# Biases and second weights of a 48-expert layer: VectorE adds the second bias, the second weights are read in 512-byte runs, six sets of weights

## The chip, the cores and the metric

The kernel runs on one core of a Trainium2 chip. A core has five engines that work side by side, each on its own queue of instructions in order: TensorE (PE, matmuls; its weight loads are shown apart as PEld), VectorE (DVE), ScalarE (ACT), GpSimd (POOL) and SyncE (SP, which only issues transfers here). Sixteen DMA engines move data between HBM and SBUF. The engines meet by semaphores. The metric is the device time of one execution in microseconds (us), as the median of several runs; lower is better.

## The reference, cut to what matters

The model is a stack of four layers, each an attention-like block and a feed-forward block, with a layer norm around each. The change lies in the feed-forward block of the second layer, a mixture of experts in which each of 48 experts picks its own 128 of 4096 tokens of width 256:

```python
E, S, D, M = (48, 4, 256, 256)      # W1: (E, S, D, M), b1: (E, S, M), W2: (E, S, M, 64), b2: (E, S, 64)
logits = xf @ Wr.T
vals, idx = jax.lax.top_k(logits.T, cap)          # cap = 128
w = jax.nn.softmax(vals, axis=-1)
xg = xf[idx]
h = jax.nn.gelu(jnp.einsum('ecd,esdm->ecsm', xg, W1) + b1[:, None], approximate=False)
y = jnp.einsum('ecsm,esmk->ecsk', h, W2) + b2[:, None]
y = y.reshape(E, cap, D) * w[..., None]
out = jnp.zeros_like(xf).at[idx.reshape(-1)].add(y.reshape(-1, D))
```

All of it is in float32. Each expert has four slices (S). A slice takes all 256 inputs to 256 hidden units, and these to its own 64 of the 256 outputs. So the first weights of an expert are 1 MB and the second 256 KB.

## The kernel before, in words

`tile_sandwich_kernel` runs the layers one after another over 8 sequences of 512 tokens, `X`, which stay in SBUF. Tiles come from pools. A pool with `bufs=n` hands out n buffers in turn for each tag, and an instruction that writes a buffer waits until the last readers of its former contents are done. The order on each engine's queue is made by a scheduler from the program and these dependences. Transfers on one queue are issued in that order, so one that waits holds up those behind it.

The routing runs inside the attention block of the same layer (`class Choice`). For each sequence `logits` normalizes the tokens, writes them to HBM as `xn_d` (L1156) and multiplies them by the router. `lists` sorts each expert's best tokens and writes them to HBM as `tab_d` (L1195). `l1_ffn` does this for the last sequence, number 7, then calls `slots`. That merges the sorted lists on VectorE: offsets `ati` (L1272), ownership masks `own` (L1290 to L1293), five indirect loads `win` from `tab_d` issued by GpSimd (L1277), products `v` (L1299 to L1302), and small matmuls `pgot` that give the token numbers `iT` and weights `wT` of all experts (L1307, L1309).

Then comes the loop over the 48 experts, in which every engine has a part:

- SP issues the loads of the expert's first weights `w1` (L1350), second weights `w2` (L1351) and second bias `b2` (L1352) into one of three sets of buffers. In `w1` the 256 inputs lie on 128 partitions in two halves `c`. In `w2` the 256 hidden units lie on the partitions in the same way, unit c x 128 + p on partition p, so that a run of consecutive bytes in HBM is one row of 64 numbers, 256 bytes.
- GpSimd issues the indirect load of the 128 tokens, `xg` (L1354).
- PE transposes them into PSUM, `pxg` (L1359), and VectorE copies them to SBUF, `xgT` (L1361).
- PE multiplies: 16 matmuls give the hidden units `h`, eight blocks of 128 units by 128 tokens, four in each half (L1368). In the trace a float32 matmul is two PE instructions with a weight load each, a transpose is one. The stationary side of a matmul (`lhsT`) is loaded first and is called the weights by PE; here it is a block of `w1`.
- ScalarE adds the first bias and applies gelu, `hT` (L1373). The bias is a column of `b1`, which lies in the layer's slot of small weights; the slot is handed to the next layer's feed-forward weights `l2f_gu` (L250) once `b1` is no longer read. These are integers, which VectorE turns into floats in six pieces (L1798).
- PE starts the output `y` with a matmul of a row of ones and the row `b2`, which sets the bias in all 256 columns (L1377), and adds eight matmuls of 64 columns (L1379), two for each slice.
- VectorE multiplies by the tokens' weights, `yw` (L1383), and GpSimd issues an indirect transfer that adds the 128 rows to `out_d` in HBM (L1384).

After the experts `l2_attn` begins: `late` loads the sums of a sequence back as `yl` (L1504) and adds them to `X`. Its tiles take the SBUF space of the experts' pools, and its first instructions (L1420, L1429, L1442) wait for the last of the transfers that add rows.

Of the kernel before, what the change touches and what calls it, by code (L numbers as in the profile page):

```python
# [9 lines left out]
F32 = mybir.dt.float32  # L10
# [4 lines left out]
ALU = mybir.AluOpType  # L15
# [4 lines left out]
P = 128  # L20
# [3 lines left out]
D = 256  # L24
# [1080 lines left out]
class Choice:  # L1105
# [7 lines left out]
    E, NL, K = 48, 10, 128  # L1113
# [212 lines left out]
def l1_ffn(K):  # L1326
    nc, tc = K.nc, K.tc
    b1 = K.W["l1_ffn"][:, 96:480]
    ch, i = K.choice, K.i
    E = ch.E  # L1330
    with ExitStack() as es:
        es.enter_context(ch.es)

        def pool(name, bufs, **kw):
            return es.enter_context(tc.tile_pool(name="f1" + name, bufs=bufs, **kw))
        cst = pool("c", 1)
        wp = pool("w", 3)
        sb = pool("s", 2)
        pmm = pool("pm", 2, space=PSUM)
        pH = pool("ph", 4, space=PSUM)  # L1340
        pY = pool("py", 2, space=PSUM)
        ch.logits(NB - 1, sb, pmm, "mm")
        for _ in ch.lists(len(ch.GROUPS) - 1):
            pass
        wT, iT = ch.slots(cst, sb, pmm, "mm")
        for e in range(E):
            w1 = wp.tile([P, 4, 2, D], F32, tag="w1", name=f"w1_{e}")
            w2 = wp.tile([P, 4, 2, 64], F32, tag="w2", name=f"w2_{e}")
            b2 = wp.tile([1, D], F32, tag="b2", name=f"b2_{e}")
            nc.sync.dma_start(out=w1, in_=i["l1f_w1"][e].rearrange("s (c p) m -> p s c m", p=P))  # L1350
            nc.sync.dma_start(out=w2, in_=i["l1f_w2"][e].rearrange("s (c p) k -> p s c k", p=P))  # L1351
            nc.sync.dma_start(out=b2, in_=i["l1f_b2"][e:e + 1, :])  # L1352
            xg = sb.tile([P, D], F32, tag="xg", name=f"xg{e}")
            nc.gpsimd.indirect_dma_start(  # L1354
                out=xg, out_offset=None, in_=ch.xn_d[:, :],
                in_offset=bass.IndirectOffsetOnAxis(ap=iT[:, e:e + 1], axis=0))
            ps = pmm.tile([P, 2, P], F32, tag="mm", name=f"pxg{e}")
            for c in range(2):
                nc.tensor.transpose(ps[:, c, :], xg[:, c * P:(c + 1) * P], K.ident)  # L1359
            xgT = sb.tile([P, 2, P], F32, tag="xgT", name=f"xgT{e}")  # L1360
            nc.vector.tensor_copy(xgT, ps)  # L1361
            hT = sb.tile([P, 8, P], F32, tag="hT", name=f"hT{e}")
            for half in range(2):
                ph = pH.tile([P, 4, P], F32, tag="h", name=f"h{e}_{half}")
                for j in range(4):
                    s, m = 2 * half + j // 2, j % 2
                    for c in range(2):
                        nc.tensor.matmul(  # L1368
                            ph[:, j, :], lhsT=w1[:, s, c, m * P:(m + 1) * P],
                            rhs=xgT[:, c, :], start=(c == 0), stop=(c == 1))  # L1370
                for j in range(4):
                    q = 4 * half + j
                    nc.scalar.activation(  # L1373
                        hT[:, q, :], ph[:, j, :], AF.Gelu,
                        bias=b1[:, 8 * e + q:8 * e + q + 1])
            py = pY.tile([P, D], F32, tag="y", name=f"y{e}")
            nc.tensor.matmul(py, lhsT=K.ones, rhs=b2, start=True, stop=False)  # L1377
            for q in range(8):
                nc.tensor.matmul(  # L1379
                    py[:, (q // 2) * 64:(q // 2 + 1) * 64], lhsT=hT[:, q, :],  # L1380
                    rhs=w2[:, q // 2, q % 2, :], start=False, stop=(q == 7))
            yw = sb.tile([P, D], F32, tag="yw", name=f"yw{e}")
            nc.vector.tensor_scalar(yw, py, wT[:, e:e + 1], None, ALU.mult)  # L1383
            nc.gpsimd.indirect_dma_start(  # L1384
                out=ch.out_d[:, :],
                out_offset=bass.IndirectOffsetOnAxis(ap=iT[:, e:e + 1], axis=0),
                in_=yw, in_offset=None, compute_op=ALU.add)

    def late(b, pool):
        y = pool.tile([P, NT, D], F32, tag="xn", name=f"yl{b}")  # L1390
        nc.sync.dma_start(
            out=y, in_=ch.out_d[b * L:(b + 1) * L].rearrange("(n p) d -> p n d", p=P))
        K.add_norm(b, [y[:, n, :] for n in range(NT)], pool, parts=2)


    K.late = late
# [847 lines left out]
def l3_ffn(K):  # L2244
# [18 lines left out]
    with ExitStack() as es:  # L2263
# [295 lines left out]
        for b in range(NB):  # L2559
# [11 lines left out]

LAYERS = (("l0_attn", load_l0_attn, l0_attn), ("l0_ffn", load_l0_ffn, l0_ffn),
          ("l1_attn", load_l1_attn, l1_attn), ("l1_ffn", load_l1_ffn, l1_ffn),
          ("l2_attn", load_l2_attn, l2_attn), ("l2_ffn", load_l2_ffn, lambda K: None),
          ("l3_attn", load_l3_attn, l3_attn), ("l3_ffn", lambda K: None, l3_ffn))
# [94 lines left out]
```

## Time and profile before

| what | value |
|---|---|
| median of 3 runs | 4558.23 us (4555.81 to 4564.57) |
| the profiled execution | 4555.24 us |
| its span, first to last instruction | 4553.5 us |
| granted PE clock, mean | 0.930 |
| PE busy | 3963.8 us (87%) |
| weight loads on PE busy | 2633.7 us (58%) |
| VectorE busy | 2698.8 us (59%) |
| ScalarE busy | 2016.2 us (44%) |
| GpSimd busy | 2118.9 us (47%) |
| `h` matmuls of the experts (L1368) | 1536 instructions, 185.0 us |
| `y` matmuls of the experts (L1379) | 768 instructions, median 275 ns |
| bias matmuls of the experts (L1377) | 96 instructions, median 375 ns |
| loads of `w1` and `w2` | 48 x 1024 KB and 48 x 256 KB |

The shares of the span are averages over all layers, and each layer has its own limit. The change touches a stretch of some 300 us, and what it is worth has to be read there. Matmuls are pipelined, so their durations overlap: 275 ns each at a pace of about 110. The distance from one weight load to the next says more than the mean duration. A wait is named by the instruction that waited, and by what ended the wait. In a line of the timeline the columns are the start, the length of the group, engine, line, operation, written tile <- read tiles, shape, and how many instructions were merged. "issue" is idle time in which an engine waited for nothing that the profile shows. The strip of the DMA engines gives the busy share in tenths, with packet times that overlap counted twice.

### The profile page before, as it was taken

The numbers are of one execution on the slowest core, as the hardware profiler recorded it, in microseconds if no ns is written. First come the engines' busy times: TensorE is split into PE (matmuls) and PEld (weight loads), VectorE is DVE, ScalarE is ACT, GpSimd is POOL, SyncE is SP. The second block draws the span as 40 slices with busy tenths as digits, with TensorE's granted clock in tenths as the row PEclk, the third lists the DMA queues.
The fourth block names the chain that finished last, engine by engine and source line by source line (L and its number), as shares of the span: only waits on it lengthen the run. The fifth ranks groups of instructions, "written<-read, shape, count | busy, mean of one in ns | idle before, by whom it ended". The sixth has DMA issues, their size and how long they took to land. (4 is left out here: it accounts for less than half of the span.)

```text
span 4553.5 us, 63426 instructions
## 1 busy us (share of the span) xinstructions
PE 3963.8 (87%) x21672; PEld 2633.7 (58%) x21672; DVE 2698.8 (59%) x7145; ACT 2016.2 (44%) x4210; POOL 2118.9 (47%) x2081
## 2 busy tenths in 40 slices
PE   8868888999998599699999978998888876899997
PEld 3435765555655499544554534565655545678884
DVE  7767656456757611255566534888888899721115
ACT  5532433444344233334444444767676655311112
POOL 0045222444344244344555423889988879223321
PEclk9889999999999799889999989899999886899999
DMA  4377621000000299400000002343433334336653
GB/s 120 94 218 189 179 62 63 5 5 7 7 10 16 69 254 251 130 5 10 6 6 6 1 23 68 123 125 126 127 122 122 124 110 136 103 118 234 228 180 113
DMA packets 392818, 442.90 MB, mean 97 GB/s; under 512 B 147853, under 2 KB 275967, under 8 KB 391983
## 3 DMA queue, kind: packets, MB, share of 16 engines
q1 hardware_dynamic: 361087, 390.18, 28.4%
q0 software_dynamic: 16272, 31.87, 2.6%
q10 hardware_dynamic: 15136, 16.80, 1.1%
q8 instruction: 172, 2.82, 0.3%
q14 instruction: 151, 1.24, 0.1%
HBM read 372.49 MB, written 66.26 MB: 96 GB/s over the span
## 5 line engine op out<-in xcount | busy, mean ns | idle before, releaser
L2085 POOL TENSOR_TENSOR h<-h,C 128x1024 f32<-128x1024 f32 x256 | 613.3, 2408 | 135.3 <-DVE h L2081 87.8
L2081 DVE TENSOR_TENSOR_SCAN h<-dA,dB 128x512 f32<-128x512 f32 x480 | 568.4, 1209 | 90.2 <-ACT dA L2069 73.9
L1039 POOL TENSOR_SCALAR p<-p,rs 128x128 f32<-128x128 f32 (+3 forms) x256 | 275.8, 1085 | 417.3 <-DVE rs L1038 261.1
L2069 ACT ACTIVATE dA<-dl,A 128x512 f32<-128x512 f32 x480 | 330.3, 690 | 174.4 <-DVE h L2081 173.7
L1605 DVE CUSTOM_DVE_ANT_0 junk<-S,mask 128x256 f32<-128x256 f32 (+3 forms) x512 | 249.5, 487 | 195.0 <-PE S L1599 156.7
L2098 PE MATMUL y<-C,h 128*128 128x128 f32 x2048 | 298.4, 297 | 68.0 <-POOL h L2085 67.9
L2098 PEld LDWEIGHTS y<-C,h 128*128 128x128 f32 x2048 | 263.2, 155 | 155.3 <-POOL h L2085 98.6
L1633 ACT ACTIVATE PT<-T 128x128 f32<-128x128 f32 (+3 forms) x512 | 198.0, 435 | 278.5 <-PE T L1628 267.6
L1599 PE MATMUL S<-KZ,QT 64*128 64x512 f32 (+3 forms) x1024 | 260.9, 492 | 23.9 <-DVE mx L1605 23.6
L2297 PE MATMUL gb<-xbT,w_b 128*128 128x256 f32 (+1 forms) x1472 | 255.3, 332 | 1.0 <-ACT ts L2501 0.6
L2297 PEld LDWEIGHTS gb<-xbT,w_b 128*128 128x128 f32 x1472 | 230.4, 191 | 22.8 <-ACT ts L2501 0.8
L2303 DVE TENSOR_TENSOR hTb<-sb,gb 128x512 f32<-128x512 f32 x71 | 48.8, 687 | 325.4 <-PE gb L2297 325.4
L2064 POOL TENSOR_TENSOR dB<-du,B 128x1024 f32<-128x1024 f32 x96 | 234.0, 2437 | 0.1
L1883 PE MATMUL pf<-fT,w_l_ffn 128*128 128x512 f32 x384 | 208.3, 681 | 26.5 <-ACT fT L1877 10.4
L1628 PE MATMUL T<-QT,KZ 64*128 64x384 f32 (+3 forms) x1024 | 216.7, 464 | 2.9 <-ACT PT L1633 2.5
L2064 DVE TENSOR_TENSOR dB<-du,pb 128x1024 f32<-128x1024 f32 x160 | 191.2, 1195 | 23.0 <-ACT pb L2062 21.2
L182 POOL TENSOR_TENSOR X<-X,yn 128x256 f32<-128x256 f32 (+1 forms) x56 | 79.4, 1436 | 255.3 <-ACT yn L177 213.9
L1373 ACT ACTIVATE hT<-h,w_l_ffn 128x128 f32<-128x128 f32 x384 | 109.5, 368 | 197.9 <-PE h L1368 197.9
L1368 PE MATMUL h<-xgT,w 128*128 128x128 f32 x1536 | 185.0, 279 | 0.0
L1636 POOL TENSOR_SCALAR_AFFINE_SELECT PT<-PT 128x512 f32<-128x512 f32 x128 | 81.2, 634 | 219.8 <-ACT PT L1633 206.8
L1599 PEld LDWEIGHTS S<-KZ,QT 64*128 64x128 f32 x1024 | 117.2, 193 | 113.9 <-issue 58.4
L2534 POOL DMA_INDIRECT ys<-yb,place x71 | 69.8, 984 | 238.7 <-ACT yb L2533 224.5
(605 smaller groups left out, 9266.5 us busy)
## 6 DMA issues: line engine op xcount, KB each, us to landing
w_b<-l3f_w SPq DMA_DIRECT2D x138, 512.0 KB
C<-xdd SPq DMA_DIRECT2D x256, 256.0 KB
B<-xdd SPq DMA_DIRECT2D x256, 256.0 KB
w<-l1f_w SPq DMA_DIRECT2D x48, 1024.0 KB
w<-l1f_w SPq DMA_DIRECT2D x48, 256.0 KB
band<-l0fd SPq DMA_DIRECT2D x30, 320.0 KB
X<-x SPq DMA_DIRECT2D x16, 512.0 KB
c<-ys SPq DMA_DIRECT2D x16, 512.0 KB
```

What stands on the lines that cost most here:

```text
L1039: nc.gpsimd.tensor_scalar(p[:, 0:n], p[:, 0:n], rs, None, ALU.mult)
L1599: nc.tensor.matmul(ps[:, 0:n], lhsT=QT[half, qt * P:n], rhs=KZ[half, j % 2, 0:n], start=True, stop=True)
L1605: nc.vector.tensor_tensor_reduce(out=junk[:, 0:n], in0=ps[:, 0:n], in1=mask[:, L - n:L], scale=1.0, scalar=-3.0e38, op0=ALU.add, op1=ALU.m ...
L1628: nc.tensor.matmul(ps[:, 0:n], lhsT=KZ[half, j % 2, kt * P:(kt + 1) * P], rhs=QT[half, kt * P:L], start=True, stop=True)
L1633: nc.scalar.activation(PT[:, j, :], ps[:, 0:n], AF.Exp)
L1883: nc.tensor.matmul(ps, lhsT=gu[:, k, j * 768 + c * P:j * 768 + (c + 1) * P], rhs=R[b]["fT"][:, k, :], start=(k == 0), stop=(k == 1))
L2064: on.tensor_tensor(dBs[k], R[b]["du", h], B[:, None, :].to_broadcast([P, 2, L]), ALU.mult)
L2069: nc.scalar.activation(dA, R[b]["dl", h][:, c, :], AF.Exp, scale=A[:, 2 * h + c, n:n + 1])
L2081: nc.vector.tensor_tensor_scan(hs[k][:, c, :], dA, dBs[k][:, c, :], 0.0, ALU.mult, ALU.add)
L2085: nc.gpsimd.tensor_tensor(hs[k], hs[k], row_C.pop(k)[:, None, :].to_broadcast([P, 2, L]), ALU.mult)
L2098: nc.tensor.matmul(R[b]["y", h][q // 2][:, q % 2, c * P:(c + 1) * P], lhsT=t[:, c, q * P:(q + 1) * P], rhs=K.ident, is_transpose=True, sta ...
L2297: nc.tensor.matmul(ps[:, q, :], lhsT=ww[:, k, (c + q) * P:(c + q + 1) * P], rhs=xT[:, k, :], start=(k == 0), stop=(k == 1))
```

## The change

Five edits, all in `l1_ffn`:

- The pool of the experts' weights has six sets of buffers in place of three.
- The second weights are loaded as `(p c) k`: hidden units 2p and 2p + 1 lie on partition p, and their two rows of 64 numbers are one run of 512 bytes.
- For this the blocks of hidden units change: block m of a slice has units m, m + 2, m + 4 and so on. So the `h` matmuls take every second column of `w1` as weights, `m::2`, and the first bias has to be rearranged in the same way. Two tiles do that once, before the loop: `turn`, made of the even or odd columns of the identity matrix on GpSimd, and `bq`, the rearranged bias, made by four matmuls with `turn` on PE (the tiles `pbq`) and two copies on ScalarE.
- The second bias is loaded into all 128 partitions, 128 KB in place of 1 KB. The matmul with the row of ones is gone; each pair of matmuls of a slice now starts and ends its own sum in PSUM.
- VectorE adds the bias from SBUF to `y` (`tensor_tensor`), and multiplies by the tokens' weights in a second instruction.

```diff
@@ -1334,7 +1334,7 @@
         def pool(name, bufs, **kw):
             return es.enter_context(tc.tile_pool(name="f1" + name, bufs=bufs, **kw))
         cst = pool("c", 1)
-        wp = pool("w", 3)
+        wp = pool("w", 6)
         sb = pool("s", 2)
         pmm = pool("pm", 2, space=PSUM)
         pH = pool("ph", 4, space=PSUM)
@@ -1342,14 +1342,27 @@
         ch.logits(NB - 1, sb, pmm, "mm")
         for _ in ch.lists(len(ch.GROUPS) - 1):
             pass
+        turn = cst.tile([P, 2, 2, P], F32, name="turn")
+        nc.gpsimd.memset(turn, 0.0)
+        bq = cst.tile([P, 4 * E, 2], F32, name="bq")
+        for c in range(2):
+            for half in range(2):
+                nc.gpsimd.tensor_copy(
+                    turn[:, c, half, 64 * half:64 * half + 64], K.ident[:, c::2])
+            pb = pmm.tile([P, 4 * E], F32, tag="mm", name=f"pbq{c}")
+            for half in range(2):
+                nc.tensor.matmul(
+                    pb, lhsT=turn[:, c, half, :], rhs=b1[:, half::2],
+                    start=(half == 0), stop=(half == 1))
+            nc.scalar.copy(bq[:, :, c], pb)
         wT, iT = ch.slots(cst, sb, pmm, "mm")
         for e in range(E):
             w1 = wp.tile([P, 4, 2, D], F32, tag="w1", name=f"w1_{e}")
             w2 = wp.tile([P, 4, 2, 64], F32, tag="w2", name=f"w2_{e}")
-            b2 = wp.tile([1, D], F32, tag="b2", name=f"b2_{e}")
+            b2 = wp.tile([P, D], F32, tag="b2", name=f"b2_{e}")
             nc.sync.dma_start(out=w1, in_=i["l1f_w1"][e].rearrange("s (c p) m -> p s c m", p=P))
-            nc.sync.dma_start(out=w2, in_=i["l1f_w2"][e].rearrange("s (c p) k -> p s c k", p=P))
-            nc.sync.dma_start(out=b2, in_=i["l1f_b2"][e:e + 1, :])
+            nc.sync.dma_start(out=w2, in_=i["l1f_w2"][e].rearrange("s (p c) k -> p s c k", c=2))
+            nc.sync.dma_start(out=b2, in_=i["l1f_b2"][e].partition_broadcast(P))
             xg = sb.tile([P, D], F32, tag="xg", name=f"xg{e}")
             nc.gpsimd.indirect_dma_start(
                 out=xg, out_offset=None, in_=ch.xn_d[:, :],
@@ -1366,21 +1379,21 @@
                     s, m = 2 * half + j // 2, j % 2
                     for c in range(2):
                         nc.tensor.matmul(
-                            ph[:, j, :], lhsT=w1[:, s, c, m * P:(m + 1) * P],
+                            ph[:, j, :], lhsT=w1[:, s, c, m::2],
                             rhs=xgT[:, c, :], start=(c == 0), stop=(c == 1))
                 for j in range(4):
                     q = 4 * half + j
                     nc.scalar.activation(
                         hT[:, q, :], ph[:, j, :], AF.Gelu,
-                        bias=b1[:, 8 * e + q:8 * e + q + 1])
+                        bias=bq[:, 4 * e + q // 2, q % 2:q % 2 + 1])
             py = pY.tile([P, D], F32, tag="y", name=f"y{e}")
-            nc.tensor.matmul(py, lhsT=K.ones, rhs=b2, start=True, stop=False)
             for q in range(8):
                 nc.tensor.matmul(
                     py[:, (q // 2) * 64:(q // 2 + 1) * 64], lhsT=hT[:, q, :],
-                    rhs=w2[:, q // 2, q % 2, :], start=False, stop=(q == 7))
+                    rhs=w2[:, q // 2, q % 2, :], start=(q % 2 == 0), stop=(q % 2 == 1))
             yw = sb.tile([P, D], F32, tag="yw", name=f"yw{e}")
-            nc.vector.tensor_scalar(yw, py, wT[:, e:e + 1], None, ALU.mult)
+            nc.vector.tensor_tensor(yw, py, b2, ALU.add)
+            nc.vector.tensor_scalar(yw, yw, wT[:, e:e + 1], None, ALU.mult)
             nc.gpsimd.indirect_dma_start(
                 out=ch.out_d[:, :],
                 out_offset=bass.IndirectOffsetOnAxis(ap=iT[:, e:e + 1], axis=0),
```

## The prediction

> **What bounds the kernel now.** I read the page first (the order by time and the strip of slices), then the stretch in which the 48 experts run, by engine. The stage runs from about 1579 us (first `h` matmul) to 1882 us (last `y`), 303 of the 4553.5 us of the span. Busy time by engine in its middle (the columns are the stretch, its length, then busy us of PE, weight loads, VectorE, ScalarE, GpSimd, then clock, DMA share, GB/s):
>
> ```profile
> core 0: us, PE busy (x) PEld busy (x) DVE busy (x) ACT busy (x) POOL busy (x), PEclk, DMA share, GB/s
> 1600.00:1850.00 250.00, 250.00 (x2068) 232.30 (x2067) 35.41 (x78) 91.23 (x320) 101.50 (x79) 1.00 0.95 251
> ```
>
> PE never rests, and the DMA engines read 0.95: two candidates for the bound. Who waits for whom tells them apart. In the waits of that stretch no PE instruction waits for a weight load, and the SP queue's own waits from 1440 to 1900 us show the opposite, loads waiting for PE to free one of three buffers:
>
> ```profile
> SPq L1350 <- PE h L1368: 149.7, 45, 31.3
> ```
>
> The DMA share adds packet times that overlap. One period of 6.30 us, by packets, and two short stretches in it that hold one kind alone (1 KB runs of `w1`; 256-byte runs of `w2`):
>
> ```profile
> DMA  9577799999999999999998999999999996410014
> ```
> ```profile
> DMA packets 602, 0.62 MB, mean 385 GB/s; under 512 B 0, under 2 KB 602, under 8 KB 602
> ```
> ```profile
> DMA packets 592, 0.17 MB, mean 278 GB/s; under 512 B 591, under 2 KB 591, under 8 KB 591
> ```
>
> The strip has a hole at the end of each period, and 1 KB runs move at 385 GB/s where the mean is 251. So PE's order sets the period. One expert on the weight-load queue (start, length, row):
>
> ```profile
> 1703.45 1.20 PEld L1379 LDWEIGHTS y<-w,hT 128*128 128x128 f32 x10
> 1704.52 0.20 PEld L1359 LDWEIGHTS pxg<-C,xg 128*128 128x128 f32 x1
> 1704.63 0.31 PEld L1379 LDWEIGHTS y<-w,hT 128*128 128x128 f32 x2
> 1704.80 0.19 PEld L1359 LDWEIGHTS pxg<-C,xg 128*128 128x128 f32 x1
> 1705.12 0.29 PEld L1377 LDWEIGHTS y<-b,ones 1*128 1x128 f32 x2
> 1705.74 0.52 PEld L1379 LDWEIGHTS y<-w,hT 128*128 128x128 f32 x4 [0.33 <-issue]
> 1706.18 3.65 PEld L1368 LDWEIGHTS h<-xgT,w 128*128 128x128 f32 x32
> ```
>
> The reader is to see the pace, 32 loads in 3.57 us (1706.18 to 1709.75), 0.11 us each whether the matmul behind has 128 or 64 columns, and the one break in it: from the second `pxg` load to the next `y` load takes 0.94 us, with only the bias pair in between.
>
> **The change, part by part.**
>
> *Bias matmul off PE.* Without L1377 the `y` load would follow `pxg` after 0.11 us: 0.94 - 0.11 = 0.83 us an expert. The biases of experts 0 and 1 ran early (1513.8), outside the stage, so 46 experts: 46 x 0.83 = 38.2 us, all on the path.
>
> *What is late next.* In the instruction order of the changed kernel the experts go in pairs: both pairs of transposes sit in the tail of the odd expert's `y`. From the second `pxg` load of the even expert to its first `h` load lie six loads, 0.66 us. `xgT` needs 0.43 until VectorE starts (1704.80 to 1705.23 here), 0.42 to copy and some 0.05 to be seen: 0.90. So PE waits 0.24 us in each of 23 pairs: 5.5 us lost. Inside a pair the second `xgT` is long done. Gain left: 32.7 us, a period of 6.30 - 0.83 + 0.12 = 5.59.
>
> *Bias on VectorE.* The one `yw` (0.48) becomes an addition from PSUM (0.42, the L853 group of the same shape) and a product from SBUF (0.41, L1514): +0.35 an expert. VectorE is busy 35 of 250 us and GpSimd 101, so it lies beside PE for 47 experts: the next `yw` buffer and PSUM buffer are a period away. It counts once, at the end: +0.35. No instruction but the scatter stands behind it.
>
> *Weights strided.* `w1[:, s, c, m::2]` takes every second column: 32 loads an expert with 8-byte steps. No row of before has that on PE. Bounds, from the groups by form:
>
> ```profile
> L1368 PEld LDWEIGHTS h<-xgT,w 128*128 128x128 f32 x1536 | 178.0, 194 | 0.0
> L661 PEld LDWEIGHTS pf<-band,Vw 128*64 128x64 f32 x480 | 54.5, 198 | 98.6 <-issue 64.0 <-DVE gt L618 10.1 <-POOL s L674 9.9
> L885 PEld LDWEIGHTS po<-at,u 128*64 128x64 f32 x256 | 13.0, 135 | 10.5 <-DVE u L861 4.7 <-DVE at L835 0.6
> L1299 DVE TENSOR_TENSOR v<-win,own 128x128 f32<-128x128 f32 x5 | 1.5, 293 | 5.1 <-DMA win<-tab_d,ati 4.9
> ```
>
> Contiguous loads cost 135 ns for 64 columns and 194 for 128: 0.92 ns a column over some 76. L661 steps 1 KB from column to column and costs 198 for 64: 1.9 a column, twice. So the upper end is a doubled pace, 0.11 x 32 = 3.6 us an expert, 171 us. The lower end is 0; a faster load than a contiguous one is excluded, since the columns are the same. The nearest row by step is L1299, which reads `win` in 8-byte steps: 293 ns against 287 for a contiguous product of that shape (L1542). I take 0.
>
> The Trainium skill ("SBUF — State Buffer", the note on cachelines under the port swizzle) says that SBUF has 16-byte lines, that two hits a line hide the access, and that each change of line pays. Eight-byte steps make two hits a line: free by the first half, which agrees with L1299. Read by the last half it speaks against the change: L661 changes line at every column, a contiguous load at every fourth, so 0.98 ns is three quarters of a change, and a step of 8 bytes adds a quarter, 0.33 ns x 128 x 32 = 1.3 us an expert; the sum would then be about 30 us slower instead of 35 faster.
>
> *DMA.* An expert now moves `w1` (1.05 MB at 385 GB/s: 2.72 us), `w2` (0.26 MB: 0.94 at 278 GB/s; 0.68 if 512-byte runs go like 1 KB runs, the bounds), gather and scatter (23.1% of 6.3: 1.46). The bias load grows from 1 KB to 128 KB, 0.34 us. Before 5.12 us, after 5.20 to 5.46: under 5.59, and hidden by PE while six sets run ahead.
>
> *Six sets, and the front.* The new order on SP is `w1`, `w2` of expert 0, then `xn_d` of batch 7 (1525.6 here), then all else of sets 0 to 5, then the last `tab_d` (1553.3), then `b2` of 5. Sets 1 to 5 are 7.2 MB; the stretch 1505 to 1518 moved sets at 297 GB/s: 24 us, done near 1551. `tab_d` lands by 1556; its reader starts at 1564.2. Nothing lost. `turn` (GpSimd, before the X addition at 1518.2), four matmuls and two ScalarE copies fall in 1514 to 1532, where those engines wait for batch 7's chain: 0, and about 3 us if that cover were gone.
>
> *A load that the diff doesn't show.* `b1` is now read only by the early `pbq` matmuls, so the load of `l2f_gu` into the same slot (1.5 MB, L250) moves from the stage's end to just behind `b2` of 5, near 1554.6. At the end it was in the way:
>
> ```profile
> 1881.39 0.37 SPq L250 DMA_DIRECT2D w_l_ffn<-l2f_gu  x1
> ```
> ```profile
> 1882.72 1.55 POOL L1384 DMA_INDIRECT out_d<-yw,iT  x1 [3.80 <-DVE yw L1383]
> 1888.96 0.42 POOL L1420 MEMSET mask<- 128x384 f32 x1 [4.69 <-DMA out_d<-yw,iT]
> ```
>
> The last scatter took 6.2 us to land against a median of 3.9: -2.3 us for all that follows. Its six conversions (L1798, 0.42 each) move too, into VectorE's queue between `ati` (1563.05) and the first `v` (1567.28): 2.5 + 0.82 for `own` ends at 1566.4, hidden by the `win` gather with 0.9 us to spare. One left the chain after `yl`: -0.4.
>
> *Sum.* -38.2 + 5.5 + 0.35 - 2.3 - 0.4 = -35.0. The profiled execution took 4555.24 (span 4553.5 and 1.7 around it): 4520. The median of the runs shown, 4558.23, lies 3.0 above it.
>
> **The rivals.**
>
> *A, strided loads cost* (slower). Decides from 35.0 us / 1536 loads = 23 ns a load. Full doubling gives 4555 + 171 - 35 = 4691; half of that 4606. For: every large-step row (L661's matmul too, 646 ns against 380 for contiguous 256 columns). Against: L1299.
>
> *B, transfers become the bound.* If the 0.95 share is real work, an expert has 5.98 us of it now and 5.98 - 0.26 + 0.34 = 6.06 after (6.32 if 512-byte runs gain nothing). Period 6.06 saves 0.24 x 46 = 11; three more sets loaded ahead take 3 x 3.7 = 11 out of the stage; the end gives 2: 4531, or 4542. For: the share. Against: the hole and 385 GB/s.
>
> *C, the front is late.* If sets 1 to 5 move at 210 GB/s, as in the stretch of the lone `xn_d` (1526 to 1528.5, its idle edges counted in), they end at 1560, `l2f_gu` near 1569, and VectorE holds `own`, `v` and `iT` behind the conversions, some 6 to 10 us: 4526 to 4530. Against: five sets follow one another without such edges.
>
> **How the numbers follow.** The forecast 0.65, A 0.18 (0.15 at more than 23 ns), B 0.11, C 0.06. About 0.2% is what a measurement of this kernel can tell from no change. Faster: 0.65 + 0.11 + 0.06, less a little of B's slow end: 0.80; within 0.2%: 0.04; slower 0.16. The likeliest case's own range is 4510 (no wait at the pairs, 5.5, and 4 of run spread) to 4531 (conversions or pairs twice as dear). The range goes up past B to 4552, which takes in loads dearer by up to 20 ns; most of A is left out.
>
> **What would show it.** Right: no L1377 rows, 50 loads a period of about 5.6 us, `h` loads still 0.11 us apart, PE waiting for `xgT` about 0.24 us at each second expert, the last scatter landing in about 4 us, `l2f_gu` issued near 1554. Wrong: `h` loads over 0.13 us apart (A); PE waiting for `w1` or `w2` with SP not waiting for PE (B); VectorE idle at L1811, the new line of the conversions, before the first `v` (C). Outside these, a stage that starts later than 1579 or a lower granted clock in it would spoil the sum.

## The result, and the profile after

The changed kernel takes 4615.55 us (median of 6 runs, 4609.99 to 4637.96) against 4559.27 us for the kernel before (6 runs beside it, 4555.81 to 4564.57): a ratio of 1.0131 with a 95% interval of 1.0116 to 1.0146. It is 56 us slower where 35 us faster was forecast. The profiled execution took 4609.99 us, its span is 4608.3.

Line numbers behind the edited block are 13 higher than before: the `h` matmuls are L1381, the `y` matmuls L1391, the addition of the bias L1395, the product with the gate L1396, the scatter L1397.

**Where the time went.** The first `h` load of the stage starts at 1581.1 us (1578.8 before) and that of the last expert at 1928.6 (1876.3). The 47 steps between them take 347.5 us where they took 297.6. So the loss of 50 us lies inside the stage of experts; the next stage's first product comes 53.2 us later than before and the last matmul of the kernel 54.8. The stage by stretches of 50 us (columns: stretch, length, busy us of PE, weight loads, VectorE, ScalarE, GpSimd, then clock, DMA share, GB/s):

```profile
1600.00:1650.00 50.00, 50.00 (x434) 49.65 (x434) 10.00 (x26) 19.44 (x68) 20.74 (x16) 1.00 1.03 287
1650.00:1700.00 50.00, 47.01 (x408) 46.25 (x406) 9.62 (x24) 18.51 (x65) 20.07 (x16) 1.00 1.01 278
1700.00:1750.00 50.00, 40.28 (x308) 39.68 (x307) 6.44 (x16) 14.65 (x52) 14.66 (x12) 0.86 0.72 204
1750.00:1800.00 50.00, 41.16 (x284) 40.60 (x285) 7.21 (x18) 12.31 (x44) 14.87 (x12) 0.80 0.66 184
```

There are two halves. In the first 50 us the change does what it should: PE is never idle and does 434 instructions where it did 414. Then it falls off, and from 1700 us on PE rests for a fifth to a quarter of the time, the granted clock reads 0.80 to 0.86, and the DMA engines, which were full (1.03), carry a third less. So it isn't a throughput that the stage ran into: everything is slower at once.

The weight-load queue in the first half, for two experts (start, length, row):

```profile
1605.94 3.84 PEld L1381 LDWEIGHTS h<-xgT,w 128*128 128x128 f32 x32
1609.71 1.20 PEld L1391 LDWEIGHTS y<-w,hT 128*128 128x128 f32 x10
...
1617.51 0.66 PEld L1381 LDWEIGHTS h<-xgT,w 128*128 128x128 f32 x5
```

From the 32 loads at 1605.94 to those of the next pair of experts at 1617.51 are 11.57 us, 5.785 an expert. The forecast was 5.59. The 32 strided loads take 3.77 us (1605.94 to 1609.71), 118 ns each, where the contiguous ones took 112: 32 x 6 ns = 0.19 us an expert, which is the difference.

Who waits for whom from 1580 to 1900 us (waiting instruction, what it waited for, us in all, times, the longest), first the engines, then the SP queue:

```profile
DVE yw L1395 <- DMA out_d<-yw,iT: 180.8, 31, 9.3
POOL out_d L1397 <- DVE yw L1395: 162.9, 31, 8.1
...
PEld pxg L1372 <- DMA xg<-xn_d,iT: 50.1, 18, 5.4
```
```profile
SPq L1365 <- DVE yw L1395: 155.1, 34, 8.6
SPq L1363 <- PE h L1381: 74.0, 24, 30.9
```

VectorE's addition, which the forecast put beside PE at no cost, waits 180.8 us for scatters to land. In the kernel before, the same place (`yw` at L1383) waited for nothing but `y` (1580 to 1880 us):

```profile
DVE yw L1383 <- PE y L1379: 44.5, 47, 8.2
```

And PE's weight-load queue waits for gathered tokens, 50.1 us, which it did not before. For weights PE doesn't wait in this stretch. On SP, the load of the second bias (L1365) waits 155.1 us for the addition; the 1 MB of `w1` and the 256 KB of `w2` of the next set are queued behind it.

The scatters themselves, from the tile's view, in 1585 to 1690 and in 1750 to 1900 us:

```profile
L1397 POOL DMA_INDIRECT out_d<-yw,iT x16: 1567/1612/1640, 1590.9 to 1685.2; - x16
...
DMA to landing us min/median/max: 3.9/5.6/7.0
```
```profile
L1397 POOL DMA_INDIRECT out_d<-yw,iT x17: 1571/1618/1627, 1752.4 to 1897.1; - x17
...
DMA to landing us min/median/max: 7.4/8.3/9.4
```

Before, over the whole stage:

```profile
DMA to landing us min/median/max: 3.7/3.9/5.8
```

In 1585 to 1690 us the median of before was 4.2. All scatters add into one sum `out_d`, so each waits for the one before it: in the changed kernel no scatter is issued sooner than 0.77 us after the landing ahead of it, and most exactly then. Before, landing and these 0.8 us made 4.7 us of a period of 6.30. Now scatters follow each other at 6.3 us (1590.9 to 1685.2, 15 steps), where PE's period is 5.79, and later at 9.0 (1752.4 to 1897.1, 16 steps). One cycle of the second half (start, length, row; in brackets the idle time before and what ended it):

```profile
1742.98 0.42 DVE L1395 TENSOR_TENSOR yw<-y,b 128x256 f32<-128x256 f32 x1 [6.88 <-DMA out_d<-yw,iT]
...
1743.43 0.34 SPq L1365 DMA_DIRECT2D b<-l1f_b  x1
...
1743.67 1.57 POOL L1397 DMA_INDIRECT out_d<-yw,iT  x1 [7.82 <-DVE yw L1395]
...
1743.87 0.38 SPq L1363 DMA_DIRECT2D w<-l1f_w  x1
...
1744.34 0.53 SPq L1364 DMA_DIRECT2D w<-l1f_w  x1
...
1745.54 1.02 POOL L1367 DMA_INDIRECT xg<-xn_d,iT  x1 [0.30 <-issue]
...
1746.86 0.98 POOL L1367 DMA_INDIRECT xg<-xn_d,iT  x1 [0.30 <-PE h L1381]
...
1751.70 0.42 DVE L1395 TENSOR_TENSOR yw<-y,b 128x256 f32<-128x256 f32 x1 [7.91 <-DMA out_d<-yw,iT]
...
1752.24 0.47 PE L1372 MATMUL pxg<-C,xg 128*128 128x128 f32 x1 [4.61 <-DMA xg<-xn_d,iT]
...
1752.39 1.62 POOL L1397 DMA_INDIRECT out_d<-yw,iT  x1 [4.54 <-DVE yw L1395]
```

The landing of a scatter frees a `yw` buffer at 1742.98; the addition runs; its end frees a bias buffer, and SP issues the next bias and `w1` (1.2 MB) at 1743.43 and 1743.87, and here `w2` too at 1744.34, in the same microsecond as GpSimd issues the next scatter (1743.67). That scatter lands 8.0 us later, at 1751.70, and the round begins again.

Two things in these rows are easily misread. The row of the scatter names the addition as what it waited for. But in the order of the experts this scatter is that of expert 22 and the addition that of expert 23: the product that the scatter sends had ended at 1734.4. It waited for the landing ahead of it, and so did the addition. And the way from the scatters to PE leads over GpSimd's queue. The gathers of experts 26 and 27 (1745.54 and 1746.86) are issued behind this scatter, although PE had read their two buffers empty by 1735.6, and at 1752.24 PE waits for the first of them. PE's idle time in the 347.5 us is 47.3 us, nearly all of it in such waits; in the kernel before it has none there.

My reading at this point: a chain of scatters that has become longer than PE's period, made worse by its own stall. The runs had to tell this from a stage held by its bytes, from the strided loads, and from the new order of the experts.

The end of the stage, where the forecast had a gain of 2.3 us:

```profile
1933.15 1.90 PE L1391 MATMUL y<-w,hT 128*128 128x64 f32 x16
...
1938.74 1.56 POOL L1397 DMA_INDIRECT out_d<-yw,iT  x1 [3.00 <-DMA out_d<-yw,iT]
...
1942.71 0.42 POOL L1433 MEMSET mask<- 128x384 f32 x1 [2.41 <-DMA out_d<-yw,iT]
```

The last scatter lands in 3.9 us as forecast, but it is issued 3.7 us after the end of the last `y` (0.8 before), because it too waits for its predecessor: the gain is eaten.

### The profile page after: what moved, and what is told of

Read it like the earlier page. It is cut to its first block, busy times and chain, and to the rows that moved or that the text cites. A ratio compares the mean times of both kernels' runs of the same rounds, so it can differ in the third digit from the quotient of the medians.

```text
span 4608.3 us, 63254 instructions
## 1 busy us (share of the span) xinstructions
PE 3974.4 (86%) x21584; PEld 2654.6 (58%) x21584; DVE 2713.2 (59%) x7193; ACT 2018.5 (44%) x4212; POOL 2123.8 (46%) x2086
## 5 line engine op out<-in xcount | busy, mean ns | idle before, releaser
L1381 PE MATMUL h<-xgT,w 128*128 128x128 f32 x1536 | 221.1, 302 | 0.0
L1386 ACT ACTIVATE hT<-h,bq 128x128 f32<-128x128 f32 x384 | 109.7, 369 | 238.6 <-PE h L1381 238.6
L1381 PEld LDWEIGHTS h<-xgT,w 128*128 128x128 f32 x1536 | 207.9, 214 | 0.7 <-issue 0.2
```

The costliest lines, as they stand in the source:

```text
L1381: nc.tensor.matmul(ph[:, j, :], lhsT=w1[:, s, c, m::2], rhs=xgT[:, c, :], start=(c == 0), stop=(c == 1))
```

## The experiments

All stage lengths below are from the first `h` load of the first expert to that of the last, 47 steps, in the profiled execution; the kernel before has 297.6 us, the changed kernel 347.5.

### Two sums

```diff
-                out=ch.out_d[:, :],
+                out=(ch.out_d, ch.out_e)[e % 2][:, :],
```

with `out_e` set to zero like `out_d`, and the next stage loading both and adding them in a `yield`ed piece of its own.

> The changed kernel, but even experts scatter-add into one sum and odd experts into a second, and the next stage adds the two when it loads them. Theory 'scatter chain': in the changed kernel each scatter-add waits for the landing of the one before it (5.4 to 8.3 us) and 0.7 us of issue, which is more than TensorE's 5.79 us per expert; with two sums a chain has two experts' time (11.57 us) for one such cycle of up to 9.0 us, so the stage keeps the 5.79 us per expert of its first experts to the end: 46 x (6.30 - 5.79) = 23.5 us less than before, and some 2 us more for the second load and the addition: about 4538. Rival 'transfers': the stage of the changed kernel is held by the bytes that all queues move, and a second sum takes none away: 4610 or more. Rival 'strided weight loads' or 'the pair order of the experts': nothing in these is changed, so 4610 as well.

Measured: 4559.07 us. The stage is 272.7 us long, every pair from the second to the last takes 4.88 + 6.69 us, and PE is busy for 50.00 us of each stretch of 50 between 1600 and 1850. The total can't be read: the next stage is written out in counted pieces, the `yield` added made one piece more of each sequence's preparation, and for seven sequences the last piece was left out (25 of 32 products `va`). So the run stands for the stage alone, and there it bears out the chain and nothing else: same bytes, same strided loads, same order in pairs.

The same without new pieces:

> The changed kernel with even experts' scatter-adds into one sum and odd experts' into a second, both loaded and added ahead of the next stage's first piece, with no piece more in that stage's plan. Theory 'scatter chain': the 5.79 us per expert of TensorE hold from the first pair to the last, so the last expert's h product begins at about 1854 us of the span (1876 before, 1929 in the changed kernel), and the next stage loses some 2 us for a second load and an addition of 1.2 us: 4536 to 4541. Rival 'transfers': 4600 or more. Rival 'the next stage is slowed by the second sum': stage of experts as said, but the total stays at 4550 or more.

Measured: 4553.75 us, ratio 0.9986 (0.9977 to 0.9996). The stage is 273.1 us:

```profile
1700.00:1750.00 50.00, 50.00 (x434) 49.56 (x434) 10.63 (x28) 19.28 (x68) 22.74 (x18) 1.00 1.03 293
```

Against the same stretch of the changed kernel: PE full, clock 1.00, and 293 GB/s instead of 204 at a share that is full. Scatters take 5.9 us to land on the one sum and 5.2 on the other (medians), which two chains cover. But the total is some 15 us above what I expected: the next stage took 766.7 us (1891.9 to 2658.6) against 753.9 before. The addition is 1.2 us on VectorE for each of eight sequences, and the second load lies in front of it. So the chain held the stage, and this cure costs 12.8 us elsewhere: the rival "the next stage is slowed by the second sum" is right as well.

### Three sets, and six sets alone

The changed kernel with `wp` at 3 again:

```diff
-        wp = pool("w", 6)
+        wp = pool("w", 3)
```

> The changed kernel with three sets of weights again in place of six; bias on VectorE, paired units and the 128 KB of bias per expert stay. Theory 'scatter chain': the landing of a scatter is long because the loads of weights that run far ahead stand on the same DMA engines when it is issued; with three sets fewer run ahead, landing falls towards the 3.9 us of the kernel before and 4.6 us of cycle fits under TensorE's 5.79: 4535 to 4545. If the landing does not depend on how far the weights run ahead, 4600 to 4620. Rival 'transfers': same bytes, less cover: 4615 or more.

Measured: 4640.59 us, ratio 1.0166 (1.0149 to 1.0183); stage 383.0 us. I expected 4535 to 4545, so this part of the theory fell: the landing is 5.9 us in 1585 to 1640 us, as long as with six sets (5.6). How far the weights run ahead isn't what lengthens it. With three sets the first step of over 10 us comes after 13 experts, with six after 21. I put that down to bias, `w1` and `w2` being tied to the addition three experts ahead and not six, which is argued and not shown. Six sets helped the change; they did not cause the loss.

The kernel before with six sets:

> The kernel before with six sets of weights in place of three, nothing else. Theory 'scatter chain': TensorE's period is 6.30 us, so the chain may take 5.6 us of landing and 0.7 us of issue before it shows; six sets lengthen the landing from 3.9 to 5 or so: 4555 to 4562, with a longer landing in the profile; above 4570 only if the landing passes 5.6. Rival 'transfers': same bytes as before, more cover: 4555 to 4560, landing as before.

Measured: 4562.48 us, ratio 1.0003 (0.9993 to 1.0012); landing 4.2 us (3.8 to 6.1), stage 297.6 us, 6.30 an expert throughout. Six sets do nothing by themselves.

### The bias on VectorE alone

The kernel before with only this part of the change, three sets, weights contiguous:

```diff
-            b2 = wp.tile([1, D], F32, tag="b2", name=f"b2_{e}")
+            b2 = wp.tile([P, D], F32, tag="b2", name=f"b2_{e}")
...
-            nc.tensor.matmul(py, lhsT=K.ones, rhs=b2, start=True, stop=False)
...
+            nc.vector.tensor_tensor(yw, py, b2, ALU.add)
```

> The kernel before with the second bias added by VectorE alone (128 KB broadcast load, sums started per output strip); weights contiguous, units in the old order, three sets. Theory 'scatter chain': TensorE's period falls to about 5.59 us (6.30 less 0.83 for the bias product and 0.12 more for the wait of a pair), so the chain has 4.9 us of landing to hide; the landing of before was 3.9 with a maximum of 5.8: 4526 to 4535 if it stays, up to 4600 if the 128 KB loads lengthen it. Rival 'transfers': 256-byte runs at the 278 GB/s seen and 128 KB more are about 5.6 us per expert: 4526 to 4535. Rival 'strided weight loads': all of the loss came from there, so the whole gain of 46 x 0.71 = 33 us shows: 4526.

Measured: 4616.52 us, ratio 1.0126 (1.0109 to 1.0143), the same as the whole change. The first pairs take 4.68 + 6.50 us, the forecast's 5.59 an expert to the digit; then the stage breaks as in the changed kernel (335.6 us), with a landing of 8.1 us in 1750 to 1900. It broke further than the 4600 that I had as the upper end. Two rivals fall: there are no strided loads here, and they can't be the loss. The order in pairs comes from this part, too, and does no harm by itself, since it holds in the runs with two sums.

### The bias product back on PE

The other way round: everything of the change, all its bytes and strided loads, but the bias added by PE.

```diff
+            nc.tensor.matmul(py, lhsT=K.ones, rhs=b2[0:1, :], start=True, stop=False)
...
-            nc.vector.tensor_tensor(yw, py, b2, ALU.add)
-            nc.vector.tensor_scalar(yw, yw, wT[:, e:e + 1], None, ALU.mult)
+            nc.vector.tensor_scalar(yw, py, wT[:, e:e + 1], None, ALU.mult)
```

> The changed kernel with the bias product back on TensorE (its first row of the broadcast tile is the factor), the scale by the gate alone on VectorE; six sets, paired units, strided loads and the 128 KB of bias per expert stay, so all bytes do. Theory 'scatter chain': TensorE's period grows to 6.30 + 32 x 0.006 = 6.49 us per expert, and a scatter may take 5.8 us to land; 1.7 MB in 6.49 us leaves the DMA engines a gap, so it lands in 4 to 5: no backlog, and a kernel with more work on TensorE is faster than the changed one by 45 us: 4560 + 46 x 0.19 + 3 of front = 4568 to 4574. Rival 'transfers hold the stage' or 'the coupling of the loads to VectorE is enough by itself': 4600 or more. Rival 'strided loads cost more than their pitch shows': above 4574 with the landing short.

Measured: 4569.26 us, ratio 1.0014 (1.0004 to 1.0024); every expert takes 6.50 us, and scatters land in 4.5 to 4.7.

```profile
1700.00:1750.00 50.00, 50.00 (x401) 46.38 (x400) 7.27 (x16) 17.64 (x62) 18.95 (x15) 1.00 0.94 259
```

PE does more work than in the changed kernel, and the kernel is 46 us faster. That is the plainest sign that PE's pace was not what held the stage. The 6.50 against 6.30 also gives the price of the strided loads by themselves: 0.20 us an expert, 9 us in all.

### One bias for all

```diff
+        b2 = cst.tile([P, D], F32, name="b2")
+        nc.sync.dma_start(out=b2, in_=i["l1f_b2"][0].partition_broadcast(P))
...
-            nc.sync.dma_start(out=b2, in_=i["l1f_b2"][e].partition_broadcast(P))
```

> The changed kernel with the second bias loaded once, from the first expert, and used for all; the loads of the other 47 are left out. It takes 128 KB of about 1.7 MB per expert off the DMA engines, and the wait of the sync engine for VectorE with them. Theory 'the landing is long because the DMA engines are full' (share 1.03 of them in the first 100 us): the share falls to 0.95, that of the kernel before, whose scatters landed in 3.9 us; landing 4 to 5, cycle 4.7 to 5.7 under the 5.79 of TensorE: 4536 to 4545. Rival 'something else lengthens the landing (the order of the experts in pairs, long runs of 1 KB)': landing stays at 5.4 or more and the stage falls behind as before: 4590 to 4615.

Measured: 4545.7 us, ratio 0.9967 (0.9954 to 0.9980); stage 284.0 us, landing 5.1 (4.9 in the first 55 us).

```profile
1700.00:1750.00 50.00, 48.81 (x423) 47.93 (x423) 10.42 (x25) 19.44 (x68) 20.86 (x16) 1.00 0.99 265
```

With 128 KB an expert less the landing comes down to PE's period less the 0.8 us to the next issue, and the collapse doesn't come; single steps still take 7 to 9 us in place of 6.69. The kernel leaves out the other 47 biases, so it serves for its time alone. It takes away two things at once, the bytes and SP's wait for VectorE; the next one takes only the second.

### The bias tiles apart

```diff
+        bp = pool("b", 10)
...
-            b2 = wp.tile([P, D], F32, tag="b2", name=f"b2_{e}")
+            b2 = bp.tile([P, D], F32, tag="b2", name=f"b2_{e}")
```

> The changed kernel with the tiles of the second bias in a pool of their own with 10 buffers, so that the sync engine need not wait for the last additions before it issues the next bias and the 1 MB of weights behind it; bytes and order are as in the changed kernel. Theory 'coupling': in the slow half of the changed kernel each scatter is issued within 0.5 us of a bias, a 1 MB and a 256 KB load that waited for the same addition, and lands behind them in 8.3 us; without the coupling the landing stays at the 5.5 us of the first half, cycle 6.2: 4565 to 4580. Rival 'full DMA engines alone': no change, 4605 to 4620.

Measured: 4595.94 us, ratio 1.0081 (1.0061 to 1.0102), with a wide spread, 4572.57 to 4608.36; the profile is of the fastest. In it SP waits 47.6 us for the addition instead of 155.1, the landing is 5.5 us even late in the stage, and most pairs go at full pace, with a collapse around 1830 us. So loosening the tie gives back some 20 us of the 56 by the medians (23 by the two ratios, 1.0131 and 1.0081), less than I expected; full engines alone, the rival, would have given nothing. Ten buffers are not enough to untie SP altogether, and there is no room for twelve: the pool of small tiles needs 32 KB a partition and would have 30.9.

### Four buffers for the weighted output

Two sums take away two waits: that of a scatter for the one before, and that of the addition for a `yw` buffer, of which there are two. This run takes away the second alone.

```diff
+        yp = pool("yw", 4)
...
-            yw = sb.tile([P, D], F32, tag="yw", name=f"yw{e}")
+            yw = yp.tile([P, D], F32, tag="yw", name=f"yw{e}")
```

> The changed kernel with four buffers for the weighted output yw in place of two; one sum, as before. Both the scatter of one expert and VectorE's addition of the next wait for the landing of the scatter before, the first because all add to one sum, the second because of the two buffers; two sums took both waits away. Theory 'the one sum': scatters still go one after another; the cycle of 9.0 us loses at most the 0.7 us in which the addition runs ahead of the scatter, and VectorE and GpSimd stall two experts later than now: 4590 to 4615. Rival 'the buffers': VectorE no longer holds the copies of the gathered tokens and the bias loads back, TensorE keeps 5.79 us: 4536 to 4545.

Measured: 4555.95 us, ratio 0.9990 (0.9980 to 1.0000); stage 288.8 us, in a profiled run of 4549.65. Both expectations miss, and the truth lies between. The waits in 1580 to 1900 us, engines and SP:

```profile
DVE yw L1396 <- PE y L1392: 132.1, 25, 7.9
...
POOL out_d L1398 <- DMA out_d<-yw,iT: 81.6, 22, 6.9
POOL out_d L1398 <- DVE yw L1397: 57.4, 13, 8.2
```
```profile
SPq L1366 <- DVE yw L1397: 12.2, 28, 0.6
```

Scatters still queue one behind another (81.6 us on GpSimd; most are again issued 0.77 us after a landing), since there is one sum. But the addition now waits for `y` alone, the bias loads wait 12.2 us in all, and late in the stage (1750 to 1900) a scatter lands in 4.8 us (median) instead of 8.3. Two kilobytes more a partition are worth some 59 us. The stage is 347.5 - 288.8 = 58.7 us shorter than that of the changed kernel, and still 288.8 - 273.1 = 15.7 longer than with two sums. This doesn't split the loss between two causes: two sums take away all 74.4 us with the two buffers as they were. The chain on one sum is in both kernels, and the four buffers shorten its cycle.

How they do it can be read from the landings, sorted by how many loads of biases or weights SP issues between 0.5 us before a scatter and 1 us after it (scatters from 1585 us to the last such load). With four buffers the median landing is 4.8 us with no such load (23 scatters), 6.0 with one (13) and 7.1 with two (4). In the changed kernel it is 4.9 (5), 6.1 (12) and 8.0 (17), and 7.9 with three (6). An addition that waits for a landing sets SP's loads beside the next scatter; one that doesn't wait leaves them where they fall.

### Versions that are faster than both

Two sums, six sets, bias on VectorE, but the old layout of the weights (contiguous loads, 256-byte runs):

> The kernel before with six sets, the second bias on VectorE and two sums, but weights in their old layout: contiguous loads into TensorE, second weights in runs of 256 bytes. Theory 'scatter chain' with strided loads at 6 ns each: period 5.79 - 32 x 0.006 = 5.59 us, 46 x 0.20 = 9 us less than the same with paired units, so about 4528 where that gives 4537. Rival 'transfers': 256-byte runs can't keep up with 5.59 us per expert (1.7 MB in 5.59 us is 304 GB/s; 296 was the most seen so far with them): the stage is held at 5.8 us or more per expert, and the total is 4537 or more.

Measured: 4542.89 us, ratio 0.9964 (0.9952 to 0.9977), 10.9 us less than with paired units. The stage is 264.2 us, 5.59 an expert from end to end:

```profile
1700.00:1750.00 50.00, 50.00 (x450) 49.64 (x449) 10.00 (x26) 20.46 (x73) 22.91 (x18) 1.00 1.11 305
```

PE never waits at 305 GB/s and a share of 1.11. So bytes were never the bound, not even in 256-byte runs. The long runs do spare the DMA engines a little (1.03 at 293 GB/s with them, some 3% less share for a byte), but nothing needs that here, and they are paid for with strided loads.

The same with three sets:

> The kernel before with the second bias on VectorE and two sums, contiguous weights and three sets. With six sets this held TensorE at 5.59 us per expert from end to end (4543). Theory 'the sets matter only for how long the chain is covered': with the chain halved three sets do as well: 4540 to 4548. Rival 'at 304 GB/s three sets cannot cover the loads': TensorE waits for w1, 4550 to 4590.

Measured: 4543.56 us, ratio 0.9962 (0.9953 to 0.9972), stage 266.3 us. Six sets are worth nothing that the total shows once the chain is covered.

The second sum merged by the DMA engines:

```diff
+        for b in range(2):
+            nc.gpsimd.dma_start(
+                out=ch.out_d[b * L:(b + 1) * L].rearrange("(n p) d -> p n d", p=P),
+                in_=ch.out_e[b * L:(b + 1) * L].rearrange("(n p) d -> p n d", p=P),
+                accum_op=ALU.add)
```

and the same for sequence `b + 2` in the next stage's first piece of `b`, in place of load and addition.

> The version with contiguous weights, six sets, bias on VectorE and two sums, but the second sum is added to the first in DRAM by eight accumulating transfers that GpSimd issues (two after the last expert, the others each two sequences ahead in the next stage), in place of a second load of 512 KB and an addition of 1.2 us on VectorE for each sequence. With the addition on VectorE the next stage took 12 us longer than in the kernel before. Theory 'it is VectorE's 8 x 1.2 us and the wait for the second load': 4530 to 4536. Rival 'GpSimd's issue and the landing of the merge cost the same': 4541 to 4550.

Measured: 4540.06 us, ratio 0.9948 (0.9931 to 0.9965): between the two expectations. The next stage takes 756.3 us, so the addition was what cost there; but its first product comes 39.7 us after the last `y`, not 29.4, since the first merge is on the path.

With the first sequence added by VectorE and the others merged:

> The version with contiguous weights, six sets, bias on VectorE, two sums and the merge by GpSimd's accumulating transfers, but for the first sequence the second sum is loaded and added on VectorE. With the merge the next stage's first product came 40 us after the last of the experts (30 in the kernel before, 34 where VectorE added for every sequence), and the stage itself took 756 us (754 before, 766 with the addition). If the wait for the first merge's landing of 10.6 us is what the 40 us hold: 34 us again with the 756 us kept, 4533 to 4536. Rival 'the merge of the second sequence or GpSimd's issue is in the way as well': 4538 to 4542.

Measured: 4531.28 us, ratio 0.9934 (0.9921 to 0.9948), 29 us faster than before. From the last `y` to the next stage's first product are 33.7 us, and that stage takes 754.0. The middle of the stage of experts:

```profile
1600.00:1850.00 250.00, 250.00 (x2238) 247.97 (x2238) 51.81 (x136) 101.73 (x357) 115.37 (x89) 1.00 1.05 285
```

PE starts 2238 instructions in the 250 us in which it started 2068 before.

## Why the prediction was wrong

*PE's order sets the period* was right of the kernel before, and stays right wherever the scatters keep up (PE busy 50.00 of 50 us in the runs with two sums).

*Bias matmul off PE, 0.83 us; what is late next, 0.24 us a pair.* Together they were right: 11.18 us a pair with contiguous weights, 5.59 an expert, as forecast. The wait of a pair is smaller, 0.17 us (the first `h` load follows the last `y` load after 283 ns in place of 112), so the bias product was worth 0.80 an expert. The stage of 264.2 us is 33.4 us shorter than before, where the two steps gave 32.7.

*Bias on VectorE* is the step that failed. It said that the addition "lies beside PE for 47 experts: the next `yw` buffer and PSUM buffer are a period away", and "No instruction but the scatter stands behind it". The next buffer is a period away only while scatters land soon enough. In 1585 to 1690 us the kernel before had a landing of 4.2 us and 0.8 to the next issue, 5.0 of a period of 6.30. A period of 5.79 left 0.8 us of slack, and a landing 1.4 us longer took it. And more stands behind: on GpSimd, behind the scatter, the gathers of the next tokens, so that PE was idle for 47.3 us; and on SP, through the bias tile that the addition frees, the next bias, `w1` and `w2`. Before the change, no load of weights or biases waited for VectorE. The copies into `xgT`, which share VectorE with the addition, were not held: each starts 0.04 us after its transposes end. Four buffers for `yw` took 58.7 us off the stage; a second sum took off all 74.4 that the chain had cost.

*DMA* was priced as throughput, 5.20 to 5.46 us an expert "hidden by PE while six sets run ahead". The throughput was right and is not the bound: 305 GB/s were carried with PE never idle. What the step left out is that fuller engines land a transfer later, and one transfer an expert is waited for. Landing went from 4.2 to 5.6 us in 1585 to 1690 as the share went from 0.95 to 1.03. The share alone doesn't give the landing: at 1.11, with two sums and contiguous weights, it was 5.7 us on the one sum and 5.4 on the other.

The Trainium skill, "DMA: Bandwidth & Descriptors", section "Rules for kernel authors", says that an accumulating DMA must wait for an earlier one on the same bytes, since nothing holds them between its read and its write. The traces agree: with one sum no scatter is issued before the one ahead of it has landed, and with four `yw` buffers GpSimd has 81.6 us of such waits. The rule says that the wait is needed; what it costs had to be measured here.

*Weights strided*, taken as 0, cost 6 ns a load: 0.195 us an expert, 9.0 us. The term was mis-sized, not the mechanism of the loss. Rival A's doubling is excluded.

The two readings of the skill's note on cachelines ("SBUF — State Buffer", under the port swizzle) gave 0 and 0.33 ns a column; the note also says that a stride of up to four fp32 is free, which the second reading passes over. Measured is 6 ns over 128 columns, 0.05. The measurement decides: neither, and nearer to the free one.

*The front* was 2.3 us later. 1.0 of that was there at 1465.8 us (logits of the sequence before the last), ahead of any of the changed lines. The conversions were not hidden as forecast. They ended at 1567.0, and `v` began at 1570.0, when `win` arrived; but `win` arrived late. GpSimd's issue of the first `win` load, at 1564.59 us, took 3.52 us while VectorE ran the conversions (1564.2 to 1567.0), where it took 1.20 before, and from `ati` to the first `v` went 5.7 us in place of 4.2. In the four runs where the conversions start just ahead of that issue (this one, both with two sums and strided loads, and the one with four buffers) it takes 3.52 us; in the four others with early conversions 1.56 to 1.62. So the term "hidden" was some 1.5 us short, a small part of the miss.

*The load that the diff doesn't show* moved as said, and the last scatter landed in 3.9 us; the wait ahead of it took the gain back.

The sum, -35.0, against the stage's own steps from run to run: +33.4 of gain with two sums and contiguous weights, less 8.9 for the strided loads (273.1 against 264.2), less 15.7 for one sum with four `yw` buffers, less 58.7 for two buffers make the stage 49.9 us longer. These are steps in this order, and not prices that hold alone. Of the rivals, B was right that the DMA engines fill up and wrong in what that does. None named the chain of scatters, though the trace of before shows its landing, up to 5.8 us, for everyone to read.

What stays open: why a landing grows with what is issued beside it, and how much of the 8.3 us is due to the bias, to `w1`, to `w2` and to the gathers. The sorted landings show the link, but no run moved one of these loads alone. Loosening the tie of the loads gave back about 20 us of the total, with a spread of 36 us between runs.

## What to carry to other kernels

When a step is made faster, list every chain that must turn once per step, scatters into one sum above all, and set its cycle (issue, landing, wake-up) against the new period, with the landing of a fuller DMA queue and not of today's. An instruction moved to an idle engine isn't free because the engine is idle: look at what its inputs' buffers free (loads queued behind that release), at what its output buffer waits for, and at what stands behind its consumer in a queue that keeps its order (here the gathers behind the scatter). When a row names what ended a wait, count which step of the loop each of the two belongs to. The cheapest mends here were two more output buffers (59 us) and a second accumulator for every other step.

## What the runs showed of the hardware that was not expected

- The landing of the accumulating scatter of 128 KB depends on what the DMA engines carry: 4.2 us at a share of 0.95 and 5.6 at 1.03 (1585 to 1690 us), and 8.3 from 1750 us on, where a bias and `w1`, 1.2 MB, are issued within half a microsecond of most of them, although the stage then moved only 180 to 198 GB/s.
- A DMA share over 1 is no sign that transfers hold a stage: 1.11 to 1.13 were kept up for 200 us with PE never idle.
- Weight loads that read every second fp32 column came 118 ns apart where contiguous ones came 112 ns apart.
- A stall costs twice: after idling the granted clock fell to 0.80 to 0.86 over 50 us, and behind the long waits for tokens, from expert 22 on, 10 to 22 of the next 32 `h` loads came 213 ns apart instead of 118.
- GpSimd's issue of an indirect load took 3.52 us beside VectorE's conversions from integers to floats, and 1.20 in the kernel before, where no conversions ran beside it.
